# Sums of the ternary down weights: from a GpSimd tree over the loaded weights to row sums taken while the weights are quantized

## The chip, the cores and the metric

The kernel runs on one core of a Trainium2 chip. A core has five engines that run side by side, each with its own queue of instructions in a fixed order: TensorE (PE, the matrix products), VectorE (DVE), ScalarE (ACT), GpSimd (POOL) and SyncE (SP, which mostly issues transfers). They wait for each other by semaphores. The metric is device time in microseconds (us), the median of several runs; lower is better.

## The reference

The reference is one decoder layer on `x` of 4 x 512 x 512: a windowed attention with 16 heads, a cross attention on a context of 4 x 1024 x 512, and a feed-forward layer with ternary weights. Only the last one matters here:

```python
def act_quant(x):        # per row, 8 bits
    scale = 128 / clip(max|x|, 1e-5)
    return clip(round(x * scale), -128, 127) / scale
def weight_quant(w):     # one scale for the matrix
    scale = 1 / clip(mean|w|, 1e-5)
    return clip(round(w * scale), -1, 1) / scale
def bitlinear(x, w):     return einsum('bsh,oh->bso', act_quant(x), weight_quant(w))
def h_bitlinear(x, w):   return einsum('bsh,oh->bso', act_quant(fwht(x)), weight_quant(w))
gate, up = bitlinear(x, w_gate), bitlinear(x, w_up)
return h_bitlinear(silu(gate) * up, w_down)   # w_down: 512 x 2048
```

## The kernel before

The kernel has three stages, one after the other.

**First stage: attention, and beside it the preparation of the weights.** The work goes in 64 units (16 row tiles of 128 rows by 4 groups of 4 heads). For each unit PE computes queries (L811), VectorE and ScalarE rotate and normalize them (`rope`, L590 to L596), POOL scales them (L817); PE turns them (L824) and forms scores (L835); ScalarE copies the scores (L840), VectorE masks them (L841) and takes the negated row maximum `nm` (L845, L846); ScalarE takes four exponentials (L854) and one of the sink (`es`, L859); VectorE forms `den` and its reciprocal (L860, L861); POOL multiplies (L862); PE turns the weights (`ptr`, L869); VectorE writes them as `pT` (L874, L879); PE multiplies by the values (L895, L901). In one turn of the main loop (L983 on) PE turns unit n, makes queries of unit n+2, scores of unit n, values of unit n-2 and `ptr` of unit n-1, and between these stand products of the projection `y` (L702). The order on PE and on ScalarE is the one in which the code is written. VectorE's, POOL's and SP's order is chosen by a scheduler when the program is built.

The generator `ternary_weights` (L708) is advanced once in every turn of that loop. After the means of the three matrices are known, it goes through gate, up and down (`n` = 0, 1, 2) in four chunks `k` of 512 x 512, each in two halves. A half is loaded as `raw` through ScalarE's queue (L748), and three VectorE operations (L756, L757, L758) scale, clip, round and write it as bf16 values -1, 0, 1 into `tern`. Transposing transfers on SP (L765) turn `tern` into `wst`, and a transfer (L770) stores it in device memory as `tern_g`, `tern_u`, `tern_d`. The tile `tern` has one buffer and `raw` two.

**Second stage: cross attention** (L1054 to L1393). It ends with the loads of the ternary weights (`ternary_load`, L1037), those of the down weights last (L1050), and with the first products of the last stage.

**Last stage: the feed-forward layer** (L1398 on). A software pipeline runs over 16 row tiles, in an order written out by hand for PE, VectorE and ScalarE: products with the gate and up weights (L396), `silu` (L401), `mid` (L405), a Hadamard transform (`mix` L381/L382, PE turns L135, products with `had` L432, butterflies on `y` L381/L382), quantization (L323, L324), a transposing transfer on SP (L478), and the product with the down weights (L494), 16 products of 128 rows of K each into one accumulator `d_ps`. POOL adds the residual (L505) for most tiles.

The quantized rows are stored as 127 minus the value, so that ScalarE's Relu (L324) does the clip, and a negative scale puts the sign right later. The product therefore has 127 times the column sum of the down weights too much, and a 17th product (L497) into the same accumulator takes it back: a 128 x 128 operand that is -127 everywhere, against `wT["sum"]`, a 128 x 512 tile whose sum over partitions is the column sum. This tile is made at the start of the last stage by four additions on POOL (L1412 to L1418): the 16 slices of `w_d`, 128 x 512 each, are added in halves, 8 + 8, 4 + 4, 2 + 2, 1 + 1, in bf16.

Of the kernel before, what the change touches and what calls it, by code (L numbers as in the profile page):

```python
# [12 lines left out]
F32 = mybir.dt.float32  # L13
F32R = mybir.dt.float32r
BF16 = mybir.dt.bfloat16
# [3 lines left out]
ALU = mybir.AluOpType  # L19
AX = mybir.AxisListType  # L20
PSUM = bass.MemoryType.PSUM

P = 128
B, T, D = 4, 512, 512
NT = B * T // P
QT = T // P
DC = D // P
# [9 lines left out]
FC = FF // P  # L37
# [15 lines left out]
def decoder_layer(  # L53
# [7 lines left out]
    nc = tc.nc  # L61
# [69 lines left out]
    def transpose_rows(pool, src, dst, tag="tr", copy=None):  # L131
# [8 lines left out]
    dram = ctx.enter_context(tc.tile_pool(name="dram", bufs=1, space=bass.MemoryType.DRAM))  # L140
# [2 lines left out]
        "u": dram.tile([P, DC, FF], BF16, name="tern_u"),  # L143
        "d": dram.tile([P, FC, D], BF16, name="tern_d"),
    }
    steps = const.tile([P, 3], F32, name="steps")
    magic = const.tile([P, 3], F32, name="magic")
    for i, value in enumerate((MAGIC, MAGIC + 127.0, 127.0)):
# [38 lines left out]
    def move(out, in_, by=None):  # L187

        (by or nc.sync).dma_start(out=out.bitcast(F32), in_=in_.bitcast(F32))
# [194 lines left out]
    class Tile:  # L384
# [104 lines left out]
        def down(self):  # L489

            self.d_ps = cdp.tile([P, D], F32, name="d_ps") if self.t != NT - 2 else \
                gup.tile([P, D], F32, tag="gu", name="d_ps")
            for f in range(FC):
                nc.tensor.matmul(  # L494
                    self.d_ps, lhsT=self.yqT[:, f, :], rhs=wT["d"][f], start=(f == 0), stop=False,
                )
            nc.tensor.matmul(  # L497
                self.d_ps, lhsT=minus_127.to_broadcast([P, P]), rhs=wT["sum"], start=False, stop=True
            )

        def result(self):
# [14 lines left out]
    with tc.tile_pool(name="aw", bufs=1) as aw, tc.tile_pool(name="akv", bufs=2) as akv, \  # L516
# [7 lines left out]
        ap = early.enter_context(tc.tile_pool(name="ap", bufs=2, side="right"))  # L524
# [36 lines left out]
        for h in range(HG):  # L561
            nc.sync.dma_start(
                out=sink_sb[h * QB:(h + 1) * QB],
                in_=sink.rearrange("(g h) -> h g", h=HG)[h].partition_broadcast(QB),
# [143 lines left out]
        def ternary_weights():  # L708
# [12 lines left out]
            for n in range(3):  # L721
                part = small.tile([P, 8], F32, tag="part", name="part", bufs=1)
                for k in range(4):
# [9 lines left out]
                    tot_ps, lhsT=ones.to_broadcast([P, P]), rhs=part, start=True, stop=True  # L733
# [9 lines left out]
            def half_chunk(n, k, h):  # L743
# [4 lines left out]
                nc.scalar.dma_start(out=raw, in_=of.rearrange("(r p) n -> p r n", p=P))  # L748
                return raw

            for n, dst in enumerate(ternary.values()):
                for k in range(4):
                    tern = ap.tile([P, 4, 512], BF16, name="tern", bufs=1)
                    for h in range(2):
                        r = half_chunk(n, k, h)
                        nc.vector.tensor_scalar(r, r, invs[:, n:n + 1], -1.0, ALU.mult, ALU.max)  # L756
                        nc.vector.tensor_scalar(r, r, 1.0, MAGIC, ALU.min, ALU.add)  # L757
                        nc.vector.tensor_scalar(  # L758
                            tern[:, 2 * h:2 * h + 2, :], r, MAGIC, None, ALU.subtract
                        )  # L760
                        yield
                    for c0 in (0, 2):
                        st = ap.tile([P, 2, 512], BF16, tag="w1", name="wst")
                        for r in range(4):
                            nc.sync.dma_start_transpose(  # L765
                                out=st[:, :, ts(r, P)], in_=tern[:, r, ts(c0 // 2, 2 * P)]
                            )
                        to = dst[:, 4 * k + c0:4 * k + c0 + 2, :] if n == 2 else \
                            dst[:, c0:c0 + 2, ts(k, 512)]
                        nc.sync.dma_start(out=to, in_=st)  # L770
                    yield

        def mask_rows():

# [159 lines left out]
        for h in range(HG):  # L934
            rows = older[h * QB:(h + 1) * QB]
            nc.gpsimd.affine_select(
                out=rows, in_=rows, compare_op=ALU.is_ge, fill=1.0, base=0,
# [5 lines left out]
            out=newer_t, in_=newer_t, compare_op=ALU.is_gt, fill=1.0, base=0,  # L943
# [93 lines left out]
    def ternary_load(which):  # L1037

        if which == "u":
            wT[which] = []  # L1040
            for i in range(2):
                w = bw.tile([P, DC // 2, FF], BF16, tag=f"qs{i}", name=f"w_u{i}")
                nc.sync.dma_start(out=w, in_=ternary[which][:, 2 * i:2 * i + 2, :])
                wT[which] += [w[:, 0], w[:, 1]]
        else:
            shape, tag = ([P, DC, FF], "ks0") if which == "g" else ([P, FC, D], "ks1")
            w = bw.tile(shape, BF16, tag=tag, name=f"w_{which}")
            for n in range(4):
                at = ts(n, shape[1] // 4)
                nc.sync.dma_start(out=w[:, at], in_=ternary[which][:, at])  # L1050
            wT[which] = [w[:, c] for c in range(shape[1])]
            wT["all"] = w

    with tc.tile_pool(name="b1", bufs=1) as b1, \  # L1054
            tc.tile_pool(name="b2", bufs=2) as b2, \
# [342 lines left out]
    with tc.tile_pool(name="c1", bufs=1) as c1, \  # L1398
# [6 lines left out]
            ):  # L1405
        had = c1.tile([P, P], F32, name="had")
        nc.scalar.dma_start(out=had, in_=c_had)
        minus_127 = c1.tile([P, 1], BF16, name="minus_127")
        nc.gpsimd.memset(minus_127, -127.0)


        w_sum = c1.tile([P, FC // 2, D], BF16, name="w_sum")  # L1412
        parts = [(w_sum, wT["all"][:, 0:8], wT["all"][:, 8:16])] + [
            (w_sum[:, 0:n], w_sum[:, 0:n], w_sum[:, n:2 * n]) for n in (4, 2, 1)
        ]
        for to, a, b in parts:
            nc.gpsimd.tensor_tensor(to, a, b, ALU.add)
        wT["sum"] = w_sum[:, 0]  # L1418

        class Nothing:  # L1420
            def __getattr__(self, name):
# [105 lines left out]
```

## Time and profile before

| | us |
|---|---|
| median of 3 runs (lowest, highest) | 1636.5 (1635.89, 1637.31) |
| profiled execution, its own time | 1637.3 |
| its span in the trace | 1635.5 |
| busy in the span: PE, DVE, ACT, POOL | 1573.3, 1173.8, 907.0, 823.2 |
| the four additions on POOL (L1417) | 1355.27 to 1371.45 |
| first and last product L497 | 1407.7, 1631.0 |
| the down weights' eight halves (L756 to L758), the last third of the preparation | 460.8 to 540.1 |

The span is what the trace covers, and 1.8 us of the profiled execution lie around it. Times in the text are us from the span's start. A line of the timeline gives start, length, engine, source line, operation, output and inputs, shapes and count; in brackets is how long the engine had been idle before it and what ended that. PEld is the load of a product's stationary operand, which overlaps the product before. An f32 product appears as two records of PE. The tenths rows cut the span in 40 slices of 40.9 us.

### The profile page before, as it was taken

What the parts mean: (1) busy time and instruction counts of PE and PEld (TensorE: products, weight loads), DVE (VectorE), ACT (ScalarE), POOL (GpSimd) and SP (SyncE); (2) the same over time, 40 slices, a digit from 0 to 9 for tenths busy, and PEclk for the clock granted to TensorE, in tenths of its full rate; (3) what the DMA queues carried; (4) which work ended last, traced back from release to release, by engine and by line L of the source; (5) the groups of instructions that cost most, each with busy time, mean ns of one, the idle gap of its engine ahead of it and who ended that gap; (6) DMA issues with size and microseconds to landing.
All of it is one profiled execution on the core that took longest, in us unless ns stands there. A gap on an engine that the chain in (4) does not pass through costs nothing.

```text
span 1635.5 us, 23068 instructions
## 1 busy us (share of the span) xinstructions
PE 1573.3 (96%) x7872; PEld 920.8 (56%) x7872; DVE 1173.8 (72%) x2250; ACT 907.0 (55%) x1888; POOL 823.2 (50%) x565
## 2 busy tenths in 40 slices
PE   7999999999999998899999999999998998999997
PEld 4566566666666565655555555555444334666664
DVE  4676987997888852755666566656565657999997
ACT  1454554555456561155444644454665665988986
POOL 2333343353444422088888888888777924011110
PEclk9999999999999999799999999999999999999999
DMA  8522313233234103221212121211111110222221
GB/s 265 153 97 77 103 54 82 73 91 83 75 88 97 39 14 81 55 65 41 47 42 60 52 48 42 59 41 47 47 59 53 34 59 9 46 46 52 46 50 41
DMA packets 127317, 106.90 MB, mean 65 GB/s; under 512 B 81268, under 2 KB 88568, under 8 KB 126776
## 3 DMA queue, kind: packets, MB, share of 16 engines
q1 hardware_dynamic: 118896, 90.85, 21.0%
q10 hardware_dynamic: 7152, 13.44, 2.8%
q0 software_dynamic: 1152, 1.15, 0.3%
q8 instruction: 62, 1.02, 0.3%
q14 instruction: 55, 0.45, 0.1%
HBM read 61.75 MB, written 10.86 MB: 44 GB/s over the span
## 4 chain that ended last, share of the span: by engine, by line
PE 82%; DVE 6%; ACT 5%; issue 3%; DMA 2%; POOL 1%; SPq 1%; DVEq 0%; POOLq 0%; ACTq 0%
PE y L702 13%; PE s_ps L1087 7%; PE st L1147 7%; PE o_ps L1183 6%; PE sc L835 4%; PE q_ps L811 3%; PE av L895 3%; PE xo_ps L1242 3%; PE q_ps L297 3%; PE st L1158 3%; PE f_ps L690 3%; PE y_ps L432 2%; PE d_ps L494 2%; PE g_ps L396 2%; PE u_ps L396 2%
## 5 line engine op out<-in xcount | busy, mean ns | idle before, releaser
L1172 POOL TENSOR_TENSOR sum<-sum,p 128x1024 f32<-128x1024 f32 x180 | 422.7, 2380 | 21.8 <-ACT p L1165 21.6
L1091 DVE TENSOR_REDUCE nm<-s_ps 128x1 f32<-128x512 f32 x480 | 301.6, 683 | 159.0 <-PE s_ps L1087 158.4
L1165 ACT ACTIVATE p<-st 128x1024 f32<-128x1024 f32 x256 | 248.0, 1019 | 93.3 <-PE st L1158 85.2
L702 PE MATMUL y<-wf,attnT 128*128 128x512 f32 x512 | 251.7, 602 | 0.0
L862 POOL TENSOR_TENSOR p<-p,den 128x512 f32<-128x512 f32 x64 | 68.2, 1065 | 261.2 <-DVE den L861 215.0
L1087 PE MATMUL s_ps<-ks,qs 99*128 99x512 f32 x480 | 188.6, 434 | 4.0 <-DVE nmT L1132 2.4
L1147 PE MATMUL st<-qs,ks 101*128 101x512 f32 x512 | 169.6, 413 | 15.6 <-ACT p L1165 13.5
L1087 PEld LDWEIGHTS s_ps<-ks,qs 99*128 99x128 f32 x480 | 83.2, 192 | 115.0 <-issue 27.3
L1183 PE MATMUL o_ps<-p,va 128*32 128x512 f32 x1024 | 138.7, 612 | 0.0
L1172 POOL TENSOR_TENSOR sum<-p,p 128x1024 f32<-128x1024 f32 x30 | 70.7, 2376 | 113.2 <-ACT p L1165 91.1
L505 POOL TENSOR_TENSOR res<-res,xres 128x512 f32<-128x512 f32 x13 | 24.3, 1872 | 200.9 <-ACT res L504 200.9
L1147 PEld LDWEIGHTS st<-qs,ks 101*128 101x128 f32 x512 | 89.3, 192 | 63.7 <-ACT p L1165 49.4
L702 PEld LDWEIGHTS y<-wf,attnT 128*128 128x128 f32 x512 | 86.1, 190 | 59.8 <-issue 59.1
L854 ACT ACTIVATE p<-s,nm 128x128 f32<-128x128 f32 x256 | 99.5, 392 | 13.9 <-DVE nm L846 13.7
L82 POOL TENSOR_TENSOR rs<-ss,neghalf 128x4 f32<-128x4 f32 (+1 forms) x72 | 78.6, 1092 | 54.1 <-DVE ss L596 47.2
L826 ACT COPY qT<-qtr 128x512 f32<-128x512 f32 x64 | 37.5, 587 | 110.0 <-PE qtr L824 110.0
L909 ACT COPY attnT<-av 128x256 f32<-128x256 f32 x128 | 42.8, 375 | 78.3 <-PE av L901 71.5
L835 PEld LDWEIGHTS sc<-kT,qT 128*128 128x128 f32 x512 | 73.0, 190 | 18.3 <-issue 15.5
L396 PEld LDWEIGHTS <-xqT 128*128 128x128 bf16 x512 | 50.4, 99 | 48.8 <-issue 3.1
L835 PE MATMUL sc<-kT,qT 128*128 128x160 f32 (+4 forms) x512 | 76.9, 293 | 0.0
L817 POOL TENSOR_TENSOR q<-q,rs 128x512 f32<-128x512 f32 x64 | 66.6, 1041 | 7.7 <-DVE q L593 2.9
L432 PE MATMUL y_ps<-had,mT 128*128 128x128 f32 x512 | 67.6, 281 | 0.1
(213 smaller groups left out, 3138.5 us busy)
## 6 DMA issues: line engine op xcount, KB each, us to landing
qs<-qH SPq DMA_DIRECT2D x128, 64.0 KB, 2.0
cx<-in_ctx SPq DMA_DIRECT2D x30, 256.0 KB, 2.9
w<-in_L_attn_out_w SPq DMA_DIRECT2D x16, 256.0 KB
w<-in_L_attn_out_w SPq DMA_DIRECT2D x4, 1024.0 KB
raw<-in_L_ffn_w_gate SPq DMA_DIRECT2D x4, 1024.0 KB, 5.3
raw<-in_L_ffn_w_up SPq DMA_DIRECT2D x4, 1024.0 KB
raw<-in_L_ffn_w_down SPq DMA_DIRECT2D x4, 1024.0 KB, 5.1
raw<-in_L_ffn_w_gate ACTq DMA_DIRECT2D x8, 512.0 KB, 3.9
```

The lines of the kernel that those rows point to most:

```text
L82: nc.gpsimd.tensor_tensor(dst, src, neghalf[:, :src.shape[1]], ALU.pow)
L396: nc.tensor.matmul(acc, lhsT=xqTs[self.t][:, c, :], rhs=w[c][:, ts(n, 512)], start=(c == 0), stop=(c == DC - 1),)
L432: nc.tensor.matmul(y_ps[:, k, :], lhsT=self.mT[q][:, k, :], rhs=had, start=True, stop=True)
L702: nc.tensor.matmul(y, lhsT=attnT[:, h, :], rhs=wf[:, h, :], start=(h == 0), stop=(h == HEADS - 1))
L835: nc.tensor.matmul(sc[:, j, lo:hi], lhsT=self.qT[:, j].rearrange("p h r -> p (h r)"), rhs=kT[:, (qt - 1) * P + lo:(qt - 1) * P + hi], star ...
L854: nc.scalar.activation(self.p[:, j, :], s[:, j, :], AF.Exp, bias=nm[:, j:j + 1], accum_out=den[:, j:j + 1],)
L1087: nc.tensor.matmul(s_ps, lhsT=qss[hh][0:R_TOP, g, ts(qt, P)], rhs=kss[b % 2][0:R_TOP, g, ts(hf, T)], start=True, stop=True,)
L1091: nc.vector.tensor_reduce(nms[m][:, g, qt, hf:hf + 1], s_ps, AX.X, ALU.max, negate=True)
L1147: nc.tensor.matmul(st[:, g % 2, :], lhsT=ks[0:R_TOP + 2, g, ts(kt, P)], rhs=qss[hh][0:R_TOP + 2, g, :], start=True, stop=False,)
L1165: nc.scalar.activation(p, st, AF.Exp)
L1172: by.tensor_tensor(sums[m][i], last[i] if kt == 1 else sums[m][i], ps[i], ALU.add)
L1183: nc.tensor.matmul(accs[m][at, :], lhsT=va[:, kt, at], rhs=ps[g // 2][:, g % 2, :], start=(kt == 0), stop=(kt == KT - 1),)
```

## The change

The column sums of the ternary down weights are no longer taken from the loaded transposed weights. While the down weights are quantized, rows of the matrix lie on partitions, and the sum that is wanted is one along each row. After each of the eight halves a VectorE reduction adds up the 512 values of a row of the chunk (128 x 2 x 512 to 128 x 2), and a ninth adds the four chunks. The 512 sums are written to device memory, `row_sums`, by a transfer on SP, one value at a time by its access pattern, and read back at the start of the last stage as one row of 512 on a single partition. The 17th product has one row of K now: -127 in a 1 x 128 operand against this row, both taken as fp32r, where it was a bf16 product with 128 rows of K. The four additions on POOL and their 8 KB per partition are gone; the memset on POOL stays, in another shape.

```diff
+    row_sums = dram.tile([QT, P], F32, name="row_sums")
...
             nc.tensor.matmul(
-                self.d_ps, lhsT=minus_127.to_broadcast([P, P]), rhs=wT["sum"], start=False, stop=True
+                self.d_ps, lhsT=minus_127.bitcast(F32R), rhs=wT["sum"], start=False, stop=True
             )
...
+            all_sums = ap.tile([P, 5, DC], F32, name="sums", bufs=1)
+            sums, total = all_sums[:, 0:4].rearrange("p k r -> p r k"), all_sums[:, 4]
             for n, dst in enumerate(ternary.values()):
                 for k in range(4):
...
                         nc.vector.tensor_scalar(
                             tern[:, 2 * h:2 * h + 2, :], r, MAGIC, None, ALU.subtract
                         )
+                        if n == 2:
+                            nc.vector.tensor_reduce(
+                                sums[:, 2 * h:2 * h + 2, k], tern[:, 2 * h:2 * h + 2, :], AX.X, ALU.add
+                            )
                         yield
...
+            nc.vector.tensor_reduce(total, sums, AX.X, ALU.add)
+            nc.sync.dma_start(out=row_sums.rearrange("r p -> p r"), in_=total)
...
-            wT["all"] = w
...
-        minus_127 = c1.tile([P, 1], BF16, name="minus_127")
+        minus_127 = c1.tile([1, P], F32, name="minus_127")
         nc.gpsimd.memset(minus_127, -127.0)
-
-
-        w_sum = c1.tile([P, FC // 2, D], BF16, name="w_sum")
-        parts = [(w_sum, wT["all"][:, 0:8], wT["all"][:, 8:16])] + [
-            (w_sum[:, 0:n], w_sum[:, 0:n], w_sum[:, n:2 * n]) for n in (4, 2, 1)
-        ]
-        for to, a, b in parts:
-            nc.gpsimd.tensor_tensor(to, a, b, ALU.add)
-        wT["sum"] = w_sum[:, 0]
+        wT["sum"] = c1.tile([1, D], F32R, name="w_sum")
+        move(wT["sum"], row_sums.rearrange("r p -> (r p)").unsqueeze(0))
```

`move` (L187) issues a transfer on SP with both sides taken as f32.

## The prediction

> **What bounds the kernel now.** I read the shares and slices first, then the chain, then the two places where the edit acts.
>
> ```profile
> PE 1573.3 (96%) x7872; PEld 920.8 (56%) x7872; DVE 1173.8 (72%) x2250; ACT 907.0 (55%) x1888; POOL 823.2 (50%) x565
> DVE  4676987997888852755666566656565657999997
> POOL 2333343353444422088888888888777924011110
> PEclk9999999999999999799999999999999999999999
> PE 82%; DVE 6%; ACT 5%; issue 3%; DMA 2%; POOL 1%; SPq 1%; DVEq 0%; POOLq 0%; ACTq 0%
> ```
>
> PE is busy for 96% of the span and has no hole in most slices, so time is won or lost only where PE waits or gets more to do. POOL's 4 in the 34th slice (1349 to 1390) is the four additions; VectorE's 8s in the 13th and 14th (491 to 573) are the stretch with the down weights. The chain in order of time names the few links that are not PE:
>
> ```profile
> 509.86 5.67 DMA raw<-in_L_ffn_w_down
> ...
> 1364.27 3.64 DVE mix L381
> 1367.92 2.52 DVE mix L382
> ```
>
> The first lies where the change adds work, the other two where it takes work away. The timeline there, by engine:
>
> ```profile
> 1363.30 8.15 POOL L1417 TENSOR_TENSOR w_sum<-w_sum 128x2048 bf16<-128x2048 bf16 x3
> 1364.27 3.64 DVE L381 TENSOR_TENSOR mix<-mid 128x512 f32<-128x512 f32 x1
> 1367.84 2.60 DVE L382 TENSOR_TENSOR mix<-mid 128x512 f32<-128x512 f32 x1
> 1370.49 0.90 PE L135 MATMUL tr_ps<-ident,mix 128*128 128x128 f32 x3 [2.19 <-DVE mix L382]
> 1371.18 1.91 PE L396 MATMUL g_ps<-w_g,xqT 128*128 128x512 bf16 x4
> 1374.18 0.60 PE L135 MATMUL tr_ps<-ident,mix 128*128 128x128 f32 x4
> ```
>
> Both `mix` operations have a twin of 0.69 us at 1377 to 1379, when POOL is idle. Here each ends just after one of POOL's tree additions does (1367.4, 1369.8), PE idles 0.61 and 2.19 us, and its next eight products take 0.43 us each instead of 0.216: the granted clock is 0.54 from 1370.5 to 1374. In the first stage:
>
> ```profile
> 515.56 0.75 DVE L756 TENSOR_SCALAR raw<-raw,invs 128x1024 f32<-128x1024 f32 x1 [1.66 <-DMA raw<-in_L_ffn_w_down]
> 516.96 0.15 DVE L860 TENSOR_TENSOR den<-den,es 128x4 f32<-128x4 f32 x1
> 517.68 0.17 DVE L861 RECIPROCAL den<-den 128x4 f32<-128x4 f32 x1
> 518.02 1.04 POOL L862 TENSOR_TENSOR p<-p,den 128x512 f32<-128x512 f32 x1 [4.15 <-DVE den L861]
> 519.12 0.66 PE L869 MATMUL ptr<-ident,p 128*128 128x128 f32 x4 [0.47 <-POOL p L862]
> ```
>
> Each attention unit runs nm (L846), four exponentials, den (L860, L861), POOL's L862, PE's ptr. The weights' work shares VectorE's queue with it. From the end of L862 to ptr the margins are, unit by unit from 496.6: 0.05, 0.39 at 503.6, 0.58 at 511.4, none at 519.12 (waited), 0.51 at 525.5, then 1.5 and 2.7. So VectorE is nearly on the path from 484 to 526.
>
> **The change part by part.**
>
> *Taken away: four additions on POOL, 16.1 us (1355.27 to 1371.45).* Without them L381 and L382 cost 0.69 each and end at 1365.64 instead of 1370.44. PE ends the products before them at 1367.2, turns `mix` in 0.43 us, does the next eight in 1.73 us at full clock, and starts the second turn at 1369.4 instead of 1373.97 (the first of its weight loads): 4.6 us won. The statistics and butterflies behind L382 on VectorE, and POOL's L108 and L82 behind the tree, come as much earlier. Lower bound 3.2 (slow products stay, at 1.4), upper 4.9 (VectorE's own loss: 2.95 plus 1.92). The rest of the last stage follows PE in a fixed order, so the shift is carried. I take 4.6.
>
> A rule disagrees on one term. The Trainium skill, "TensorE: Matmul & The Clock Gate", "What's actually happening", puts the drop to half clock after an idle window of about 3.4 us; the idle seen here was 0.61 and 2.19 us with one product between. By the rule the slow products need not be the tree's doing and the gain would be 3.2, and the whole sum below 1.4 us higher.
>
> *Added: eight reductions of 128x1024 bf16 to 128x2 on VectorE (460 to 546 us).* No bf16 reduction is in the trace. The nearest rows are the same shape in f32, and a bf16-writing pass of the same length:
>
> ```profile
> L1103 DVE TENSOR_REDUCE nm<-st 128x2 f32<-128x1024 f32 x16 | 18.6, 1218 | 1.0 <-PE st L1099 1.0
> L758 DVE TENSOR_SCALAR tern<-raw 128x1024 bf16<-128x1024 f32 x24 | 20.3, 848 | 0.2
> ```
>
> L758's best is 0.69 (its listing's median 0.694). I take 1.21, start to start 1.13, being the same operation and shape; 0.69 stays as the lower end.
>
> The Trainium skill, "VectorE: DVE Perf Modes", "The perf-mode tier table", speaks against the change here: a tensor_reduce has only the 1x mode, bf16 included. By that the price is the f32 row's; without it the 0.69 row would be as good a guess, and the sum 2 us lower.
>
> The program's order on VectorE after the change puts each reduction behind its L758, and PE's, ScalarE's and POOL's order is unchanged. I moved the rows by hand:
> - Halves 1, 2 (460 to 474). The first reduction delays the scores' work by 1.13, and half 2's L756 now stands ahead of L846 and meets POOL's L817 (such overlaps stretch L756 to 1.556): nm ends at 469.35 instead of 467.50. Exponentials and es take 1.83. The second reduction stands ahead of L860 and ends at 472.45, so L861 ends at 473.03 instead of 470.82, POOL at 474.2. PE wanted ptr at 472.79: 1.5 lost.
> - Halves 3, 4 (484 to 504). nm comes 1.0 and then 1.5 late against margins of 0.05 and 0.39: 1.2 lost.
> - Halves 5, 6 (507 to 522). L756 of half 6 stands ahead of L846 here too, and waits for its load (landed 515.5; nm ended at 513.89 before). nm ends near 517.35, the reduction again precedes L860, POOL ends at 521.8. PE wanted 519.12, and is 1.2 late by then: 1.5 lost.
> - Halves 7, 8: margins 1.5 and 2.7 cover them: 0.1.
>
> Sum 4.3. With reductions of 0.69 the same walk gives 0.5, 0, 1.8, 0, that is 2.3, since half 6's wait remains. Upper bound: eight times 1.21, 9.7. PE is busy 15.00 of 15 us in each window from 550 to 580, so nothing is given back. Idles of this length don't slow PE: after 1.76 us at 1390.39 the next eight products still took 1.06 us, as always.
>
> *The final reduction* (128x16, about 0.2 us by L860's 0.16) stands ahead of a den with 2.9 us of margin: nothing. *The store of row_sums*, 512 single values, enters SP's queue after the last tern_d store (546.40) and ahead of the cx loads (607.22): 60 us cover it. It waits there for the final reduction. Its price isn't in the trace: 1.8 us by the 8 KB nmT rows at the low end; it would have to reach the 60 us to delay a cx load. *The load of w_sum* stands on SP behind the w_d loads and ahead of the first yqT transpose (1387.21). It takes the wait for the old pools, until about 1355, which that transpose had; at 2.0 us as for 64 KB loads it is there by 1358. Its reader, the first L497, gains a wait on it, with all later products queued behind; but it runs at 1407.7. POOL's memset is 0.1 us before and after.
>
> *The sixteen L497 products* go from bf16 (0.216 to the next) to fp32r with one row. fp32r products of 512 columns follow each other in 0.235 (L1147 and L1087, 906.8 to 908.3); the first of them after another type takes 0.33. So 0.02 to 0.12 each, 0.3 to 1.9 in all. bf16 to f32 shows no extra (L396 to L432 at 1360.1), so I take 0.05: 0.8.
>
> **Sum:** 4.3 + 0.8 - 4.6 = +0.5 us. The profiled execution took 1637.3 (span 1635.5 and 1.8 around it), so 1637.8; it is 0.8 above the median of the runs, 1636.5, so I predict 1637.0. With the ends of the parts, -2.3 (2.3 + 0.3 - 4.9) to +4.2 (5.5 + 1.9 - 3.2, where 5.5 lets each of the three places be 0.4 longer): 1634 to 1641. This measurement tells 0.2%, 3.3 us, from no change.
>
> **The rivals.**
> - *Slower: every reduction lands on PE's path.* Eight times 1.21 is 9.7; 9.7 + 0.8 - 4.6 = +5.9, 1642.4. For it: VectorE is busy 14.63 of 15 us from 520 to 535. Against: ptr's margins of 1.5 to 2.9 after 530. It decides from a first-stage loss of 7.1 on.
> - *Faster: VectorE's holes take the reductions.* 7.9 us of idle lie between 492 and 546; with 0.3 lost the sum is -3.5, 1633.0 or below. Against: the holes are waits in the same chain, and two reductions stand between the exponentials and L860.
> - *The gain is not had, or fp32r costs like f32.* If another wait takes the stall's place, +5.1, 1641.6. If L497 costs like an f32 product (two passes of 0.43), 16 x 0.64 adds 10, 1647. For it: nothing in the rows around 1360 to 1375. Against: VectorE, ScalarE and the sums are there in time.
>
> **How the numbers follow.** My forecast 0.52, the slower rival 0.22, the faster 0.16, the third 0.10. Within 0.2% comes from the first, slower from the second and fourth (0.32), faster from the third. The range runs from 1632.3, a little beyond the faster rival, to the slower one's 1642.4; the forecast's own is 1634 to 1641.
>
> **What would show it.** L381 and L382 at 0.69 after the first products of the last stage, no clock below 0.9 there, and the second turn 4.6 us earlier against the stage's start. In the first stage, reductions of 1.2 us, and PE waiting for L862 near 472, 504 and 520 by 4 us in all; the last stage then starts that much later. L497 to the next product in 0.24 to 0.33. I am wrong if PE shows no such waits, or ones at each half chunk, or if the start of the last stage shows a new wait in place of the old.

## The result and the profile after

| | before | after |
|---|---|---|
| median of 22 runs each (us) | 1636.84 | 1639.31 |
| lowest, highest (us) | 1634.49, 1639.5 | 1636.17, 1643.52 |
| ratio, with its 95% interval | | 1.0016 (1.0009 to 1.0024) |

The changed kernel takes 2.6 us more (1.5 to 3.9 by the interval): surely not faster, and inside the 0.2% within which the prediction calls two kernels level. The prediction said 1637.0. The two traces show that three moves of 3 to 5 us lie behind this small difference, so most of this document is about the moves.

The added lines move the kernel's lines down: L756 to L758 are now L759 to L761, the new reduction is L765, L846 is L855, L860 and L861 are L869 and L870, POOL's L862 is L871, `ptr` L878, `mix` L382 and L383, the sixteen last products L498. From the page of the kernel after, the shares, POOL's slices and the granted clock:

```profile
PE 1578.4 (96%) x7872; PEld 920.3 (56%) x7872; DVE 1174.0 (72%) x2259; ACT 905.8 (55%) x1888; POOL 809.4 (49%) x561
POOL 2433343354434332178888888888777930011010
PEclk9999999999999999799999999999999999999999
```

POOL's 4 in the 34th slice is a 0: the tree is gone (823.2 us of POOL are now 809.4). VectorE's busy time stays, though the reductions add 9.7 us: the two `mix` operations alone, which were stretched, gave 4.9 of it back. PE has 5 us more busy time. Neither row says where the end moved; that takes fixed points in the order of PE, read in both traces.

| stretch on PE (us) | before | after | difference |
|---|---|---|---|
| first stage: first `ptr` to last `y` | 570.0 | 574.5 | +4.5 |
| second stage: last `y` to last `xo_ps` | 716.1 | 717.7 | +1.6 |
| entry of the last stage: last `xo_ps` to first `d_ps` | 50.0 | 45.2 | -4.8 |
| first `d_ps` to last `d_ps` | 226.5 | 229.2 | +2.7 |

The stretches are differences of starts as the listings give them, to 0.1 us. The second stage has no changed instruction. Over the traces of all kernels below, it took 714.6 to 718.0 us, so differences of up to 2 or 3 us between two executions are drift there, and a stretch of one trace is trusted only when others repeat it. The spans of the two traces differ by 5.1 us (1635.5 and 1640.6), twice what was timed: besides the second stage, the first `ptr` comes some 0.9 us later in the changed kernel's trace (69.0 against 68.2; 67.8 to 69.0 over all traces), and the execution that was profiled took 1642.4 us, 3.1 above its kernel's median.

The entry of the last stage, first the line before the change that the comparison starts from, then the timeline of the kernel after (start, length, engine, line, operation):

```profile
1363.15 0.60 PE L135 MATMUL tr_ps<-ident,mix 128*128 128x128 f32 x4
```

```profile
1370.10 0.60 PE L135 MATMUL tr_ps<-ident,mix 128*128 128x128 f32 x4
...
1371.22 0.69 DVE L382 TENSOR_TENSOR mix<-mid 128x512 f32<-128x512 f32 x1
1371.83 0.68 DVE L383 TENSOR_TENSOR mix<-mid 128x512 f32<-128x512 f32 x1
...
1374.15 0.60 PE L135 MATMUL tr_ps<-ident,mix 128*128 128x128 f32 x4
1374.59 1.03 PE L397 MATMUL g_ps<-w_g,xqT 128*128 128x512 bf16 x4
...
1376.31 0.60 PE L135 MATMUL tr_ps<-ident,mix 128*128 128x128 f32 x4
```

The lines from 1371.22 on are those that stood at 3.64, 2.60, a wait of 2.19 and products of 1.91 before. `mix` is at 0.69 and 0.68, no wait is noted ahead of the turns, and four products take 1.03. The same turn that came at 1374.18 comes at 1376.31, although the turn ahead of the stall ran 6.95 us late (1370.10 against 1363.15): 4.8 us were won here.

In the first stage, the waits of PE between 465 and 530 us after the change, in its timeline (the bracket is PE's idle time and what ended it):

```profile
471.81 1.13 PE L904 MATMUL av<-pT,mixed 128*128 128x256 f32 x4 [0.51 <-DVE pT L888]
...
474.85 0.66 PE L878 MATMUL ptr<-ident,p 128*128 128x128 f32 x4 [0.22 <-POOL p L871]
...
500.39 0.66 PE L833 MATMUL qtr<-ident,q 128*128 128x128 f32 x4 [1.34 <-DVE q L593]
...
507.52 0.66 PE L878 MATMUL ptr<-ident,p 128*128 128x128 f32 x4 [0.43 <-POOL p L871]
...
524.23 0.66 PE L878 MATMUL ptr<-ident,p 128*128 128x128 f32 x4 [1.59 <-POOL p L871]
```

Before, this stretch had one wait, of 0.47 us. Now there are five, 4.1 us together. The new reduction in the listing of its line (lengths in ns: least, median, greatest), and its place in VectorE's timeline for half 2:

```profile
L765 DVE TENSOR_REDUCE sums<-tern x8: 1204/1208/1221, 464.5 to 545.0; 128x2 f32<-128x1024 bf16 x8
```

```profile
471.78 1.22 DVE L765 TENSOR_REDUCE sums<-tern 128x2 f32<-128x1024 bf16 x1
472.92 0.15 DVE L869 TENSOR_TENSOR den<-den,es 128x4 f32<-128x4 f32 x1
...
473.44 0.17 DVE L870 RECIPROCAL den<-den 128x4 f32<-128x4 f32 x1
```

The reduction stands straight ahead of den, whose reciprocal POOL and then PE's `ptr` wait for. Last, the sixteen products, in the listing of line 497 before and of line 498 with the row of sums:

```profile
L497 PEld LDWEIGHTS <-minus x16: 97/98/98, 1407.5 to 1630.8; 128*128 128x128 bf16 x16
L497 PE MATMUL d_ps<-w_sum,minus x16: 379/379/379, 1407.7 to 1631.0; 128*128 128x512 bf16 x16
```

```profile
L498 PEld LDWEIGHTS d_ps<-w_sum,minus x16: 181/181/182, 1409.9 to 1635.9; 1*128 1x128 f32 x16
L498 PE MATMUL d_ps<-w_sum,minus x16: 489/497/500, 1409.9 to 1635.9; 1*128 1x512 f32 x16
  issue: 6.8, 16
```

Before the change PE's weight loads had no idle time at these products, and the load began some 0.2 us ahead of its product (1407.5 and 1407.7). Now the loads stand idle for 0.42 us ahead of each of the sixteen ("issue: 6.8, 16"), and each starts with its product (both 1409.9) instead of under the product ahead.

### The profile page after: what moved, and what is told of

Its sections match the earlier page's. It is cut to its first block, busy times and chain, and to the rows that moved or that the text cites. A ratio compares the mean times of both kernels' runs of the same rounds, so it can differ in the third digit from the quotient of the medians.

```text
span 1640.6 us, 23073 instructions
## 1 busy us (share of the span) xinstructions
PE 1578.4 (96%) x7872; PEld 920.3 (56%) x7872; DVE 1174.0 (72%) x2259; ACT 905.8 (55%) x1888; POOL 809.4 (49%) x561
## 4 chain that ended last, share of the span: by engine, by line
PE 82%; DVE 7%; ACT 5%; issue 2%; SPq 2%; DMA 2%; POOL 1%; DVEq 0%; ACTq 0%; POOLq 0%
PE y L703 12%; PE s_ps L1095 7%; PE st L1155 7%; PE o_ps L1191 6%; PE sc L844 4%; PE q_ps L298 3%; PE xo_ps L1250 3%; PE st L1166 3%; PE d_ps L495 3%; PE q_ps L820 3%; PE av L904 3%; PE y_ps L433 3%; PE g_ps L397 3%; PE u_ps L397 3%; PE f_ps L691 3%; PE tr_ps L135 2%
## 5 line engine op out<-in xcount | busy, mean ns | idle before, releaser
L871 POOL TENSOR_TENSOR p<-p,den 128x512 f32<-128x512 f32 x64 | 67.4, 1054 | 262.2 <-DVE den L870 200.9
```

## The experiments

My theory after these two traces: the change is a sum of three independent moves, +4.5 us because the reductions stand in VectorE's order ahead of the attention units' next step, -4.8 us for the tree, and +2.7 us for the sixteen products. The rival: the moves are drift, the reductions are hidden in VectorE's free time, and the products cost what the prediction gave them.

In the tables, "ratio" is to the kernel before, run beside each kernel on the same chip, with its 95% interval.

### One move at a time

First the reductions alone, on top of the kernel before; nobody reads their result:

```diff
...
+            all_sums = ap.tile([P, 5, DC], F32, name="sums", bufs=1)
...
+                        if n == 2:
+                            nc.vector.tensor_reduce(
+                                sums[:, 2 * h:2 * h + 2, k], tern[:, 2 * h:2 * h + 2, :], AX.X, ALU.add
+                            )
...
+            nc.vector.tensor_reduce(total, sums, AX.X, ALU.add)
+            nc.sync.dma_start(out=row_sums.rearrange("r p -> p r"), in_=total)
```

> The kernel before, with its tree, and with the change's eight reductions, the final one and the store added in the first stage; nobody reads the sums. Theory: the reductions stand in VectorE's order ahead of the masked scores' step and of den's, whose results TensorE waits for; the trace of the changed kernel lost 4.46 us by the end of the first stage, so this kernel is 4.4 us (3.5 to 5.5) over the kernel before: about 1641.2. Rival: what the landmarks of the first stage showed is drift between two executions and VectorE's free time takes the reductions: 0 to +1 us.

Then the tree alone taken away; the sums are zero here and in the kernels that follow from this one, which so leave the correction out of the output:

```diff
-        parts = [(w_sum, wT["all"][:, 0:8], wT["all"][:, 8:16])] + [
-            (w_sum[:, 0:n], w_sum[:, 0:n], w_sum[:, n:2 * n]) for n in (4, 2, 1)
-        ]
-        for to, a, b in parts:
-            nc.gpsimd.tensor_tensor(to, a, b, ALU.add)
+        nc.gpsimd.memset(w_sum[:, 0], 0.0)
```

> The kernel before without the tree: GpSimd sets the one row of sums to zero, and the product of bf16 by 128 rows stays, so the correction by 127 times the sums is left out of the output. Theory: the tree stretched two gated products and let TensorE's clock drop for a while, worth 4.8 us by the landmarks of the changed kernel, so 4.8 us (4 to 5.5) under the kernel before: about 1632.0. Rival: the following tiles are bound by VectorE and give most of it back: 0 to -2 us.

And on that kernel the product alone:

```diff
-                self.d_ps, lhsT=minus_127.to_broadcast([P, P]), rhs=wT["sum"], start=False, stop=True
+                self.d_ps, lhsT=minus_127.bitcast(F32R), rhs=wT["sum"], start=False, stop=True
...
+        minus_127 = c1.tile([1, P], F32, name="minus_127")
...
+        wT["sum"] = c1.tile([1, D], F32R, name="w_sum")
+        nc.gpsimd.memset(wT["sum"].bitcast(F32), 0.0)
```

> The one before it in this list (no tree, sums of zero, so the correction is left out) with the change's last part alone: the product of one row of K in fp32r in place of 128 rows of bf16. Theory: the product takes 0.43 us to the next one instead of 0.22, and its weights, which load for 0.18 us, are not hidden by the product ahead of them; 16 of them cost 2.6 us by the landmarks of the last stage (up to 5 if every tile pays its 0.37), so about 1634.6 (1634 to 1637). Rival, the prediction's: 0.05 us each, 0.8 us in all, and the rest of the last stage's loss was drift: about 1632.8.

| kernel | median (us) | ratio | first stage | entry of the last | first to last `d_ps` |
|---|---|---|---|---|---|
| before (median of those runs; trace of the first table) | 1637.1 | | 570.0 | 50.0 | 226.5 |
| reductions alone | 1641.65 | 1.0027 (1.0016 to 1.0037) | 574.8 | 50.0 | 225.1 |
| no tree | 1630.52 | 0.9956 (0.9943 to 0.9968) | 570.1 | 45.2 | 225.1 |
| no tree, one row of fp32r | 1633.47 | 0.9978 (0.9969 to 0.9987) | 570.0 | 45.2 | 228.2 |

The reductions alone cost 4.4 us by the ratio (2.6 to 6.1), and their trace puts 4.8 in the first stage and adds nothing elsewhere. The rival that VectorE's free time takes them is out. Without the tree the entry is 4.8 us shorter, the very number of the change's trace. By time the gain is larger, 7.2 us (5.2 to 9.3); the trace places 4.8 of it at the tree, and the other 2.4 in stretches whose instructions are the same. The run with the reductions alone, which keeps the tree, is also 1.4 and 1.5 us shorter than the kernel before in the last stage and the second one, so this rest goes with the executions and not with the tree.

What differs there is the clock. Near the end of the last stage PE waits 2.34 us in the trace of before and 2.33 us in the one without the tree. Behind this wait the granted clock is 0.57 in the first and 1.00 in the second (windows; the columns are the stretch, its length, the busy time of PE, PEld, DVE, ACT and POOL, the granted clock, and the DMA's share and GB/s):

```profile
1609.00:1613.00 4.00, 3.52 (x18) 3.53 (x19) 1.90 (x6) 1.59 (x3) 0.27 (x1) 0.57 0.17 66
```

```profile
1604.00:1608.00 4.00, 3.51 (x25) 2.93 (x27) 2.22 (x7) 2.54 (x5) 0.23 (x1) 1.00 0.17 66
```

Such a slow spell of 3.4 us follows this wait in six of the twelve traces and not in the other six; with the old product the stage takes 225.1 us in the two traces without it and 226.5 with it. The runs agree: those without the tree had a mean granted clock of 0.988, those of the kernel before beside them 0.985. Why the same wait slows the clock in one execution and not in another was not tested.

The kernel with the reductions alone keeps the tree, and shows the stall a second time (its timeline of PE, and its windows):

```profile
1370.89 0.33 PE L135 MATMUL tr_ps<-ident,mix 128*128 128x128 f32 x1 [0.60 <-DVE mix L382]
1373.41 0.90 PE L135 MATMUL tr_ps<-ident,mix 128*128 128x128 f32 x3 [2.20 <-DVE mix L383]
```

```profile
1370.00:1374.00 4.00, 1.20 (x6) 0.73 (x5) 3.97 (x4) 0.15 (x1) 3.84 (x3) 0.86 0.00 0
1374.00:1378.00 4.00, 4.00 (x20) 2.26 (x19) 3.78 (x6) 1.67 (x3) 2.19 (x3) 0.72 0.00 0
```

VectorE is full (3.97 of 4 us), nearly all of it with two operations that need 1.4 elsewhere, while POOL runs the tree, and PE is idle and then slow. Both traces that keep the tree show this, and none of the ten without it.

The one-row product costs 3.0 us on the kernel without the tree (1633.47 against 1630.52; 3.6 by the ratios), and 3.1 in the traces of the last stage, which ran at full clock in both. The prediction's 0.8 is out. Added up, the three runs give 4.4 - 7.2 + 3.6 = +0.8 us by their ratios, each known to about 2 us, and 4.8 - 4.8 + 3.1 = +3.1 by their traces, against 2.6 timed for the change.

### What makes the product dear: its type or its rows

I first took the type for the cause, and split each sum in two bf16 numbers:

```diff
...
+            both = ap.tile([P, 2, DC], BF16, name="both", bufs=1)
+            nc.vector.tensor_copy(both[:, 0], total)
+            nc.vector.tensor_tensor(both[:, 1], total, both[:, 0], ALU.subtract)
...
-        minus_127 = c1.tile([1, P], F32, name="minus_127")
+        minus_127 = c1.tile([2, P], BF16, name="minus_127")
...
```

> The changed kernel with each sum split in two bf16 numbers that add up to it, so that the last product has two rows of K in bf16 and not one in fp32r. Theory (the type, fp32r, makes the product dear): the 2.6 us of the last stage come back and 0 to 0.3 us stay, so 2.4 us under the changed kernel, about 1636.9, level with the kernel before. Rival (few rows of K make it dear, whatever the type): the product stays at 0.4 us and the time at that of the changed kernel, about 1639.3.

Two more kernels tell type and rows apart. The changed kernel with fp32r and 128 rows, 127 of them zero:

```diff
-        minus_127 = c1.tile([1, P], F32, name="minus_127")
+        minus_127 = c1.tile([P, P], F32, name="minus_127")
-        wT["sum"] = c1.tile([1, D], F32R, name="w_sum")
-        move(wT["sum"], row_sums.rearrange("r p -> (r p)").unsqueeze(0))
+        wT["sum"] = c1.tile([P, D], F32R, name="w_sum")
+        nc.gpsimd.memset(wT["sum"].bitcast(F32), 0.0)
+        move(wT["sum"][0:1], row_sums.rearrange("r p -> (r p)").unsqueeze(0))
```

> The changed kernel with the last product padded to 128 rows of K: 127 rows of zeros under the row of sums, weights of 128x128 in fp32r. Theory (one row of fp32r is dear, 128 rows of it are not; the type alone is not the cause): the product takes 0.23 us to the next one as the products of 99 and 101 fp32r rows do, and the 2.6 us of the last stage come back: about 2 us under the changed kernel. Rival (fp32r after bf16 is dear whatever its rows): the product stays at 0.43 us, the weights load in the open, and the time stays within 0.5 us of the changed kernel's.

And the kernel without the tree with one row of bf16:

```diff
-                self.d_ps, lhsT=minus_127.to_broadcast([P, P]), rhs=wT["sum"], start=False, stop=True
+                self.d_ps, lhsT=minus_127, rhs=wT["sum"], start=False, stop=True
...
+        minus_127 = c1.tile([1, P], BF16, name="minus_127")
+        wT["sum"] = c1.tile([1, D], BF16, name="w_sum")
+        nc.gpsimd.memset(wT["sum"], 0.0)
```

> The kernel without the tree (sums of zero, so the correction by 127 times the sums is left out), with one row of K in bf16 in place of 128 rows of bf16. Theory (fp32r with few rows is dear, bf16 is not): the product takes 0.22 us to the next one and the time is that of the kernel without the tree, about 1630.5 within 0.6 us. Rival (few rows of K make a product dear in any type): about 3 us more, as the fp32r row did, 1633.5.

| last product | base | median (us) | ratio | sixteenth `d_ps` product to the `had` products behind the next turn (us) |
|---|---|---|---|---|
| 128 rows bf16 | no tree | 1630.52 | 0.9956 (0.9943 to 0.9968) | 0.87 |
| 1 row fp32r | no tree | 1633.47 | 0.9978 (0.9969 to 0.9987) | 1.23 |
| 1 row bf16 | no tree | 1633.12 | 0.9980 (0.9971 to 0.9989) | 1.12 |
| 1 row fp32r | the change | 1639.31 | 1.0016 (1.0009 to 1.0024) | 1.23 |
| 2 rows bf16 | the change | 1639.39 | 1.0015 (1.0006 to 1.0024) | 1.12 |
| 128 rows fp32r | the change | 1636.18 | 1.0004 (0.9995 to 1.0012) | 0.89 |

The last column is worked out from the timeline at each kernel's first tile with a `d_ps`: the start of the `had` products, less the start of the row of `d_ps` products and 0.2155 us for each of its products but the last. It repeats to 0.01 us at the twelve tiles behind. PE's rows at this product in the timeline without the tree, and those with one row of bf16, show why it grows:

```profile
1402.51 0.10 PEld L497 LDWEIGHTS <-minus 128*128 128x128 bf16 x1
1402.72 0.38 PE L497 MATMUL d_ps<-w_sum,minus 128*128 128x512 bf16 x1
1402.72 0.57 PEld L135 LDWEIGHTS tr_ps<-ident,mix 128*128 128x128 f32 x4
1402.93 0.60 PE L135 MATMUL tr_ps<-ident,mix 128*128 128x128 f32 x4
```

```profile
1404.85 0.09 PEld L497 LDWEIGHTS <-minus 1*128 1x128 bf16 x1 [0.42 <-issue]
1404.85 0.39 PE L497 MATMUL d_ps<-w_sum,minus 1*128 1x512 bf16 x1
1405.16 0.42 PEld L135 LDWEIGHTS tr_ps<-ident,mix 128*128 128x128 f32 x4 [0.23 <-issue]
1405.17 0.66 PE L135 MATMUL tr_ps<-ident,mix 128*128 128x128 f32 x4
```

With 128 rows the weight load runs 0.21 us ahead of its product, under the one before. With one row it starts together with its product, and so does the load of the turn behind it, which has 128 rows again: the change from 128 rows to one and the change back each leave a load uncovered. (Not every change does: products of 99 and 101 rows in turn, at 906.8 to 908.3 in the trace of before, keep 0.235 us from one to the next.) The product itself is no longer (0.39 against 0.38). So the rows are the cause: 0.25 us for a product of one or two rows of bf16, 0.36 for one row of fp32r, whose load takes 0.18 instead of 0.09, and 0.02 for 128 rows of fp32r.

Sixteen times 0.25 to 0.36 is 4.0 to 5.8; 2 to 3 of it reach the end. From the first to the last `d_ps`, traces at full clock take 225.1 us with 128 rows of bf16, 227.1 with one or two rows of bf16 and 228.2 with one row of fp32r; those with one slow spell take 226.5 before, 226.2 with the padded product and 229.2 after the change (the tied kernel below, padded too, has two and 228.2). By the medians it is 3.0 for fp32r and 2.6 for bf16 (the latter across two chips), by the padded kernel's ratio 1.9, with intervals that touch. The rest is taken up by waits: laid side by side, product by product, the kernels without the tree, with 128 rows of bf16 and with one of fp32r, part by 0.36 us at each of the first fourteen of the sixteen, 5.1 in all, and come together by 2.0 again at eight later places where PE or its loads had waited.

My theory of the type was wrong in both its forms: neither two rows of bf16 nor one row of bf16 came free, at 0.25 us each against 0.36. The padded product, the one thing in this group that keeps the row of sums and loses its price, showed that the type alone is cheap. The split in two numbers had another cost besides: its first stage takes 576.3 us, 1.8 more than the change's, with a new wait of 1.3 us ahead of a `ptr`.

The Trainium skill, "TensorE: Matmul & The Clock Gate", "Why this matters for your kernels", says that a product with 32 rows of K takes as long as one with 128. The lengths here agree (0.39 against 0.38), but its neighbours pay 0.25 us, which the page doesn't count; the measurement decides.

### What makes the reductions dear: the work or its place

The changed kernel with one reduction for a whole chunk, in the chunk's third turn, which has no other VectorE work:

```diff
-                        if n == 2:
-                            nc.vector.tensor_reduce(
-                                sums[:, 2 * h:2 * h + 2, k], tern[:, 2 * h:2 * h + 2, :], AX.X, ALU.add
-                            )
...
+                    if n == 2:
+                        nc.vector.tensor_reduce(sums[:, :, k], tern, AX.X, ALU.add)
```

> The changed kernel with one reduction of 128x2048 for each down chunk, in the chunk's third turn, which has no other VectorE work, in place of two of 128x1024 behind the ternary operations of its two halves. VectorE's work is the same: four reductions of about 2.35 us. Theory (place decides: a reduction costs when it stands right behind three long operations and ahead of den's or the maximum's step): two or three of the four still stand ahead of such a step, each 2.35 us late against a slack of 1 to 1.5, so the first stage loses 2 to 4 us and not 4.5: 0.5 to 2.5 us under the changed kernel. Rival (the work as such decides, wherever it stands): the same time as the changed kernel, within 0.5 us.

The third operation of the down chunks moved to ScalarE, which adds the rows up as it goes:

```diff
...
+                        else:
+                            for i in range(2):
+                                nc.scalar.activation(
+                                    tern[:, 2 * h + i, :], r[:, i], AF.Identity,
+                                    bias=less_magic, accum_out=sums[:, 2 * h + i, k:k + 1],
+                                )
...
```

> The changed kernel with the third operation of the down chunks (take away the magic number, round to bf16) on ScalarE, 16 instructions of 128x512 that add up their rows as they go, in place of 8 operations of 0.85 us and 8 reductions of 1.21 us on VectorE; ScalarE, which is busy for half of that time, gets 16 of about 0.77 us. Theory (VectorE's order ahead of den and the maximum makes the first stage's loss): the 4.5 us of the first stage come back and perhaps a little more, since half a down chunk is 2.1 us lighter than after the change and 0.85 us lighter than before it: 4 to 5 us under the changed kernel, about 1634.5 to 1635.5. Rival (the load moves to ScalarE, whose exponentials stand in the same chain): half of it or less comes back: 0 to 2 us under the changed kernel.

And the padded kernel with the reduction in the third turn, tied behind the last step of nm and behind den's reciprocal of that turn:

```diff
...
+                        with tc.issue_after(steps_of["nm"].ins), tc.issue_after(steps_of["den"].ins):
+                            nc.vector.tensor_reduce(sums[:, :, k], tern, AX.X, ALU.add)
...
```

> The changed kernel with the product padded to 128 rows, and with one reduction of 128x2048 for each down chunk in its third turn, tied behind the last step of the maximum of the scores and behind den's reciprocal of that turn, so that it stands while ScalarE makes the exponentials (4 of 0.58 us). VectorE's work is that of the earlier run with the third turn, four of 2.27 us. Theory (what is behind the reduction in VectorE's order decides, not the work as such): of the first stage's 4.5 us, 1 to 2.5 stay, so 2 to 3.5 us under the padded kernel, about 1633 to 1634. Rival (VectorE is full in this part of the stage, so every reduction costs wherever it stands): the first stage loses 4.5 to 5.3 us again and the time is the padded kernel's, 1636.2.

| kernel | median (us) | ratio | first stage (us) |
|---|---|---|---|
| the change | 1639.31 | 1.0016 (1.0009 to 1.0024) | 574.5 |
| third turn | 1638.86 | 1.0015 (1.0006 to 1.0025) | 575.3 |
| third operation and sums on ScalarE | 1680.36 | 1.0265 (1.0251 to 1.0279) | 615.2 |
| padded product | 1636.18 | 1.0004 (0.9995 to 1.0012) | 574.6 |
| padded product, third turn, tied | 1632.78 | 0.9981 (0.9971 to 0.9991) | 571.4 |

The third turn alone changed nothing, as its rival said: the first stage even takes 0.8 us more. The timeline of that kernel shows why this didn't speak for the rival:

```profile
519.64 0.16 DVE L867 TENSOR_TENSOR den<-den,es 128x4 f32<-128x4 f32 x1
519.76 2.29 DVE L775 TENSOR_REDUCE sums<-tern 128x4 f32<-128x2048 bf16 x1
521.97 0.17 DVE L868 RECIPROCAL den<-den 128x4 f32<-128x4 f32 x1
...
522.31 1.04 POOL L869 TENSOR_TENSOR p<-p,den 128x512 f32<-128x512 f32 x1 [6.62 <-DVE den L868]
...
523.40 0.90 PE L876 MATMUL ptr<-ident,p 128*128 128x128 f32 x3 [2.91 <-POOL p L869]
```

The reduction was set between the two steps of den, and PE waited 2.91 us for its end. The other three stood ahead of nm or between its steps. And the wait was followed by a slow clock, which the change's own first stage nowhere has (window of this kernel):

```profile
523.00:527.00 4.00, 3.60 (x11) 2.61 (x12) 2.79 (x7) 0.58 (x1) 2.39 (x3) 0.57 0.39 115
```

A spell of 3.4 us at half clock costs some 1.7 us (an estimate from the clock's 0.57 over 4 us), so of this kernel's 5.3 us about 3.6 would be left without it, which the theory had allowed. The tied kernel does the same four reductions of 2.27 us, with only their neighbours changed:

```profile
474.29 0.66 DVE L854 TENSOR_SCALAR nm<-nm,nsink_sb 128x4 f32<-128x4 f32 x1
474.86 2.27 DVE L776 TENSOR_REDUCE sums<-tern 128x4 f32<-128x2048 bf16 x1
477.06 0.67 DVE L882 TENSOR_TENSOR pT<-ptr,either_t 128x512 f32<-128x512 f32 x1
...
478.66 0.16 DVE L868 TENSOR_TENSOR den<-den,es 128x4 f32<-128x4 f32 x1
```

Here it runs from 474.86 to 477.1 while ScalarE makes this unit's exponentials (475.12 to 476.95), and den comes after. Of the first stage's 4.6 us, 1.4 remain, and the time falls by 3.4 us against the padded kernel. So the place decides, not the amount of work.

The waits of PE from 440 to 640 us in the tied kernel (total, times, longest):

```profile
PE av L903 <- DVE pT L882: 1.2, 1, 1.2
...
PE ptr L877 <- POOL p L870: 0.7, 1, 0.7
```

Next in line is `pT`, which now stands behind the reduction.

The kernel with ScalarE missed both expectations by 40 us. Its listing of the moved line:

```profile
L769 ACT ACTIVATE tern<-raw,less_magic x16: 705/714/722, 463.4 to 578.4; 128x512 bf16<-128x512 f32 x16
  DVE raw L762: 42.1, 8
```

ScalarE's order is written by hand in this stage, and it stood idle eight times for VectorE's second operation, 42.1 us in all, with the attention's own copies and exponentials behind it. PE waited 32.7 us for ScalarE's `qT` copies, and its clock fell behind these waits too (0.90 on average from 460 to 580). The work was lighter for VectorE by 16 operations; what cost the time was a wait in a queue whose order was fixed. I had priced ScalarE's work and not the wait at its head.

### A version that beats both

The last experiment takes the two lessons together: no tree on POOL, no product of few rows, nothing added to the first stage. The tree's sums are made by TensorE, by 16 products of the identity with the down weights, put where PE waits anyway:

```diff
...
+        sum_ps = cdp.tile([P, D], F32, tag="d_ps", name="sum_ps")
+
+        def add_up(f0, f1):
+            for f in range(f0, f1):
+                nc.tensor.matmul(
+                    sum_ps, lhsT=ident_b, rhs=wT["d"][f], start=(f == 0), stop=(f == FC - 1)
+                )
...
+                add_up(0, 3)
                 now.turn(0)
+                add_up(3, 6)
                 now.turn(1)
...
             prev.inner(1)
+            if s == 2:
+                add_up(6, 9)
...
             now.gated_mm(3)
+            if s == 2:
+                add_up(9, FC)
             prev.outer(2)
+            if s == 2:
+                nc.vector.tensor_copy(w_sum, sum_ps)
```

> The kernel before with the tree moved to TensorE: 16 products of the identity by the down weights, summed in the bank that holds d_ps later, which give the tree's 128 partial rows; VectorE copies them to bf16 once; the last product of each tile is the old one, of 128 rows of bf16. The products stand where TensorE waits in the kernel without the tree (0.78 and 0.68 us ahead of the first two turns, 0.72 ahead of the third tile's first turn, 1.76 ahead of its last): 3 + 3 + 3 + 7 of them at 0.216 us. Theory (the tree cost 4.8 to 6.6 us, and the 3.5 us of products lie mostly in those waits): 4 to 6 us under the kernel before, about 1631 to 1633. Rival (a product put in a wait moves the next one's start, since ScalarE and VectorE follow TensorE there): the 3.5 us and the copy's 0.7 come on top of the kernel without the tree, 1634.7.

It took 1632.23 us against 1636.71, a ratio of 0.9971 (0.9961 to 0.9981): 4.7 us under the kernel before and some 7 under the change, in the range the theory gave. Two of the four places in PE's timeline:

```profile
1354.29 0.81 PE L1417 MATMUL sum_ps<-w_d,ident_b 128*128 128x512 bf16 x3 [0.78 <-DVE xres L1247]
...
1382.83 1.67 PE L1417 MATMUL sum_ps<-w_d,ident_b 128*128 128x512 bf16 x6
1384.75 0.66 PE L135 MATMUL tr_ps<-ident,mix 128*128 128x128 f32 x4 [0.25 <-ACT mT L136]
```

At the second of the two the kernel without the tree waited 1.76 us, and 0.25 of that are left. The entry of the last stage takes 45.9 us, 0.7 more than without the tree, for 3.5 us of products: most of them lie in the waits. The first place was badly chosen: the three products wait for the same `xres` as the turn behind them and run after it, and their 0.65 us are about the 0.7 that the entry lost. (A few records of products are missing from the trace.)

## Why the prediction was right or wrong

The time, 1637.0, missed by 2.3 us and lies in the forecast's own range of 1634 to 1641. By its steps:

- **Taken away.** Right: 4.6 us predicted, 4.8 in the trace of the change and in that of the tree alone. Two `mix` operations at 0.69 and 0.68, no wait behind them, and no clock below 0.9 there, as it asked for. In both traces that keep the tree, the clock fell after waits of 0.6 and 2.2 us; in the ten without it no slow spell lies there, and after the change the next products took 1.03 us for four at once. Two traces do not show that the clock falls every time: a wait of 2.3 us later in the stage slowed it in six of twelve. The prediction set the Trainium skill's rule from "TensorE: Matmul & The Clock Gate", "What's actually happening", beside this (an idle window of about 3.4 us, a gain of 3.2): the sum by the row held, the one by the rule did not. Two readings were off, without a part in the sum. Of the eight products behind the stall six took 0.43 us and the last two 0.22. And that idles of this length don't slow PE holds for the 1.76 us it was read from, but not for the waits of 2.33 and 2.91 us above.
- **Added.** Right in size: 4.3 predicted, 4.5 in the trace, 4.4 from the run with the reductions alone. The reduction took 1.208 us where 1.21 was taken; "VectorE: DVE Perf Modes" of the Trainium skill, section "The perf-mode tier table", gives this operation no faster mode for bf16, and the length agrees. The places were only half right. At halves 1 and 2 the waits are 0.51 and 0.22, not 1.5; at halves 5 and 6 they are 0.43 and 1.59, for 1.5; and at halves 3 and 4, where `ptr` was to wait 1.2 for POOL, it is the turn of the queries, L833, that waits 1.34 for VectorE's L593. The walk by hand followed one chain and overlooked a second reader of VectorE's queue, and its errors balanced: that the sum came out so close is partly luck.
- **The final reduction, the store and the load.** Nothing, as predicted. The store of 512 single values landed after 8.6 us and not 1.8, at 560 us, and the first cx load comes well behind it. The price was wrong and the cover of 60 us held. No product waits for the load of `w_sum`.
- **The sixteen products.** This is the step that failed. It gave 0.05 us for each and 0.8 in all, with 1.9 as the upper bound; the runs show 0.36 for each where PE sets the pace, and 1.9 to 3.1 in all. The step had looked at the type and priced it by products of 99 and 101 rows and by the passage from bf16 to f32 with 128 rows. The type is indeed cheap (0.02 with 128 rows). The number of rows was taken for free, although it falls from 128 to 1. The trace of before had a better row, which the step overlooked: L1158, a group of four fp32r products of 32 rows side by side, stands between products of 101 and 128 rows in the second stage. From its timeline there:

```profile
1335.02 0.73 PE L1147 MATMUL st<-qs,ks 101*128 101x512 f32 x2 [0.18 <-ACT p L1165]
1335.68 0.19 PEld L1158 LDWEIGHTS st<-qL,kL 32*128 32x128 f32 x4 [0.36 <-issue]
1335.68 0.50 PE L1158 MATMUL st<-qL,kL 32*128 32x512 f32 x4
1336.11 0.16 PEld L1183 LDWEIGHTS o_ps<-p,va 128*32 128x32 f32 x8 [0.24 <-issue]
```

The load of L1158 starts with its product, after 0.36 us of "issue", and the load behind it shows 0.24: the same two gaps, and 0.43 us from one product to the next, as at L498 after the change. In the first stage L901, products of 64 rows between such of 128, has them as well (0.33 and 0.33 at 456.0 and 456.7). Read as a price the row would have given about 0.3 each (an estimate: 0.43 in place of 0.216 to the next, and 0.1 for the late start), 5 us, and a sum of +4 to +5 before the tiles' own waits.
- **The sum.** 4.3 + 0.8 - 4.6 = 0.5 was predicted, 4.5 + 2.7 - 4.8 = 2.4 is what the three stretches show, and 2.6 was timed. The difference is nearly all in the products' term. That 2.4 and 2.6 agree so well is in part chance, with drift of 2 to 3 us in the traces.
- **The rivals.** Not every reduction lands on the path: 4.5 of 9.7 us do. VectorE's holes do not take them all, but the rival named the right question, for with a forced order they take all but 1.4 us. The gain of the tree was had. The price of an f32 product, 0.64 more each, was not reached, but of all guesses on that term it pointed the right way.

## What to carry to other kernels

A product with few rows of K between products of 128 rows leaves two weight loads uncovered, its own and the next one's; padding it with rows of zeros was cheaper than shortening it (0.02 us against 0.36). What an added operation costs on an engine that others wait for is decided by the instruction behind it in the queue: the same four reductions cost the first stage 5.3 us where they stood ahead of or among the steps of nm and den, a slow spell of the clock included, and 1.4 behind nm's last step, so look at the order before counting free time. And when sums are wanted of an operand that TensorE reads anyway, a few products with the identity in TensorE's own waits can be cheaper than a tree on GpSimd: 4.7 us here. Against the best of the VectorE versions, the padded and tied one, no difference is shown (ratios 0.9971 and 0.9981, with intervals that overlap).

## What the runs showed of the hardware that was not expected

- The uncovered weight loads: 0.25 us for one or two rows of bf16 and 0.36 for one row of fp32r, against 0.02 for 128 rows of fp32r; the length of the product's own record hardly shows it (0.385 against 0.379), only the starts of its neighbours do.
- A store of 512 single values of 4 bytes needed 8.6 us from issue to landing.
- A wait of PE of 2.33 us is followed by 3.4 us of slow clock in some executions and by none in others, and 1.4 us of the last stage go with it. The second stage differs by up to 3.4 us (714.6 to 718.0) between executions of the same instructions; by the clock records of the traces it is at half clock for 47.8 us in the longest, 41.0 in the kernel before (716.1) and 37.6 in the one without the tree (715.0), though 41.0 in the shortest too, so the clock is not all of it.
